# Pinning the SiLU activations of two state-space layers to program order in a four-layer network kernel

## The chip, the cores and the metric

The kernel runs on one core of a Trainium2 chip. The metric is the device time of one execution in microseconds (us), given as the median of three runs; the profile is that of a fourth execution. Five engines with queues of their own do the work: TensorE (PE in the profile, its weight loads apart as PEld), VectorE (DVE), ScalarE (ACT), GpSimd (POOL) and SyncE (SP), on whose queue all DMAs of this kernel are issued.

## The reference, cut to what matters

The input is 16 images of 192 channels and 32 by 32 pixels. Four layers follow each other, each as `x = x + layer(group_norm(x))`: an mLSTM block, a Mamba block, a depthwise convolution, and a two-dimensional selective scan over four directions. The two state-space layers, 1 and 3, hold the part that matters here:

```
xc = silu(depthwise_conv(x_in))                  # 384 channels, 1024 positions
dt = softplus(dt_proj(x_proj(xc)))
h_t = exp(dt_t * A) * h_{t-1} + dt_t * x_t * B_t # 16 states for each channel
y_t = sum_n h_t[n] * C_t[n]
out = layer_norm(y + D * xc) * silu(z)           # layer 3; layer 1 has no norm here
```

In layer 3 the scan runs over each image in four orders (rows, columns, and both reversed), and the four results are added.

## The kernel before, in words

**Stages.** `run` calls `layer0`, `layer12` and `layer3` one after the other. Layer 0 takes about the first 4310 us, layer 1 with layer 2 at its side the next 3800, and layer 3 the last 9830, by the times of the scan instructions of L933 in the trace.

**The scan loop.** `scan_run` walks over *units*. A unit is 512 positions of one image in one scan direction; layer 3 has 8 units for an image, 128 in all. Each unit has 16 *steps*, one for each state n, so an image of layer 3 is 128 steps, and I number them 0 to 127 below. A step holds, for each of three blocks of 128 channels,

- on ACT: `da = exp(dt * A)` (L909), and in three parts `xbt = ut * B` (L889);
- on PE: four small matmuls that turn `xbt` into the scan's layout (L917, L920), and four that add `h * C`, transposed, to the sum y (L951);
- on DVE: the scan itself, `h` (L933);
- on POOL: `h * C` for all three blocks in one instruction (L940).

The buffers between them are few: five of `da`, three of `xb`, four of `h`, two of `xbt`, four of `cb` (the row of C, which a DMA on SP spreads over 128 partitions, L891).

**Side work.** Everything else of a layer is written as Python generators that `Side.tick` advances between the parts of a step, each in a span of steps given where it is added in `layer3`. For an image b of layer 3 these are: `prep` of the next unit, in steps 16j-14 to 16j-3 (it has the softplus: Exp in L841, Ln in L842, three times for a unit); `layer3_columns` of image b-1 in steps 2 to 8; `layer3_tail` of image b-1 in steps 8 to 36; `layer3_local` and `layer3_z` of image b+1 in steps 45 to 78; `layer3_xc` of image b+1 in steps 78 to 112. The tail of the last image runs after the loop.

**The tail.** `layer3_tail` handles an image in two halves of 512 positions. For each it issues a DMA that fetches z back from DRAM into `sz`, which lives in the single buffer `tmp`; normalises v (`layer_norm`: Square L361, Ln L363, Exp L364); calls `self.silu(sz)`; scales v with three activations (L1579); and multiplies v by `sz` on POOL (L1583). After that instruction the second half's DMA (L1574) may refill `tmp`. `tmp` is also the work buffer of `layer3_front` (L1458, L1461) and of `layer3_local` (L1495).

**The activation table.** An activation needs its function's table set in ACT. SiLU is in one set; Exp and Ln are together in another, whose name the kernel keeps as `LNEXP`. The kernel writes a load of that set behind every SiLU (L531 in layer 0, L1207 in layers 1 and 3), and the compiler adds a load ahead of every activation whose function the set in force lacks. All show in the profile as ACT_TABLE_LOAD, under the line of the activation that they serve.

**What sets the order.** The kernel is written for a scheduler that takes the traced instructions and lays out each engine's queue by its own estimate of when inputs are ready; waits come from the data alone. An instruction whose input is there early may so be placed far ahead of where it was traced. Where that is not wanted, an edge can be added that only orders issue: `keep_in_program_order(ins)` puts `ins` behind the instruction traced just before it on the same engine. In `silu` (L1204) that is done for the table load, whose predecessor is the SiLU activation. So the load can't come ahead of the SiLU, but nothing holds the two together, and nothing holds the SiLU to its place. In layer 0 the SiLU activations (L529) are pinned as well. `silu` is called from `layer1_conv`, `layer1_gate`, `layer3_xc` and `layer3_tail`.

Of the kernel before, what the change touches and what calls it, by code (L numbers as in the profile page):

```python
# [11 lines left out]
AF = mybir.ActivationFunctionType  # L12
# [239 lines left out]
class Program:  # L252
# [950 lines left out]

    def silu(self, x):  # L1204

        self.nc.scalar.activation(x, x, AF.Silu)
        self.tc.keep_in_program_order(self.nc.scalar.preload_act_table_set(LNEXP))  # L1207

    def layer1_gate(self, b, bp, psum):
# [424 lines left out]
```

## Time and profile before

| what | value |
|---|---|
| median of 3 runs (lowest to highest) | 17937.86 us (17929.37 to 17949.53) |
| the profiled execution's own time | 17942.07 us |
| its span | 17940.3 us |
| PE busy | 16197.5 us (90%) |
| DVE busy | 13314.9 us (74%) |
| ACT busy | 12215.5 us (68%) |
| POOL busy | 11472.7 us (64%) |
| mean granted TensorE clock | 0.945 |
| scan of layer 3, first to last step | 8112.7 to 17879.1 us |
| one image of layer 3, typical | 611 to 617 us |

The span is the profiled part of that execution, and 1.8 us lie around it. The shares of the whole span mix stages with different loads: ACT is busy for 1166 of the 4310 us of layer 0, but for 8533 of the 9767 us of layer 3's scan, where PE is busy for 8991, DVE for 8490 and POOL for 7894. Such shares can be asked for any stretch of time, and the stretches that count here are a few steps long. In a list of groups each row gives the line, engine and operation, the count after an x, then the busy time in total, the mean duration in ns, and the idle time just before with what ended it.

### The profile page before, as it was taken

What the parts mean: (1) busy time and instruction counts of PE and PEld (TensorE: products, weight loads), DVE (VectorE), ACT (ScalarE), POOL (GpSimd) and SP (SyncE); (2) the same over time, 40 slices, a digit from 0 to 9 for tenths busy, and PEclk for the clock granted to TensorE, in tenths of its full rate; (3) what the DMA queues carried; (4) which work ended last, traced back from release to release, by engine and by line L of the source; (5) the groups of instructions that cost most, each with busy time, mean ns of one, the idle gap of its engine ahead of it and who ended that gap; (6) DMA issues with size and microseconds to landing.
All of it is one profiled execution on the core that took longest, in us unless ns stands there. A gap on an engine that the chain in (4) does not pass through costs nothing.

```text
span 17940.3 us, 264092 instructions
## 1 busy us (share of the span) xinstructions
PE 16197.5 (90%) x99836; PEld 11281.1 (63%) x99836; DVE 13314.9 (74%) x14875; ACT 12215.5 (68%) x19906; POOL 11472.7 (64%) x5556
## 2 busy tenths in 40 slices
PE   8999889898999999979899999999988999999998
PEld 4444444444655555546777777777777777777777
DVE  4444445444777777758888888888888888888888
ACT  2222222223766666647888898888888888988888
POOL 3333333333555555547787888787878877887878
PEclk8898898888999999989999999999999999999999
DMA  1111111112433333333333233333333332333232
GB/s 43 31 32 32 32 32 30 30 31 82 116 115 116 112 117 114 111 107 100 89 101 103 84 97 105 97 90 95 107 91 93 99 105 85 92 105 101 88 93 65
DMA packets 877953, 1511.12 MB, mean 84 GB/s; under 512 B 80336, under 2 KB 311197, under 8 KB 865834
## 3 DMA queue, kind: packets, MB, share of 16 engines
q1 hardware_dynamic: 876682, 1494.22, 28.6%
q8 instruction: 791, 12.96, 0.3%
q14 instruction: 480, 3.93, 0.1%
HBM read 1264.99 MB, written 228.92 MB: 83 GB/s over the span
## 4 chain that ended last, share of the span: by engine, by line
PE 27%; ACT 11%; DVE 8%; issue 4%; POOL 4%; DMA 1%; SPq 0%; POOLq 0%; DVEq 0%; ACTq 0%
PE y L951 7%; PE xb L917 6%; DVE h L933 6%; PE xb L920 4%; ACT da L909 4%; ACT xbt L889 3%; POOL h L940 3%; PE mm L1094 3%; PE mm L810 1%; PE mm L839 1%; PE mm L1517 1%; ACT L909 1%; ACT L842 1%; PE mm L1502 1%; ACT lnsq L842 1%
## 5 line engine op out<-in xcount | busy, mean ns | idle before, releaser
L940 POOL TENSOR_TENSOR h<-h,cb 128x1536 f32<-128x1536 f32 x2560 | 8880.1, 3472 | 1635.0 <-DVE h L933 1045.2
L909 ACT ACTIVATE da<-dt,neg_a 128x512 f32<-128x512 f32 x7680 | 5242.3, 714 | 1542.7 <-DVE h L933 1455.8
L933 DVE TENSOR_TENSOR_SCAN h<-da,carry,xb 128x512 f32<-128x512 f32 x3840 | 4664.9, 1262 | 812.8 <-PE xb L920 605.4
L951 PE MATMUL y<-const,h 128*128 128x128 f32 x30720 | 4739.7, 277 | 132.9 <-DVE ysum L1391 54.6
L933 DVE TENSOR_TENSOR_SCAN h<-da,xb 128x512 f32<-128x512 f32 x3840 | 4439.2, 1202 | 389.9 <-PE xb L920 255.2
L917 PE MATMUL xb<-const,xbt 128*128 128x128 f32 x23040 | 4128.4, 283 | 490.1 <-ACT xbt L889 266.7
L889 ACT ACTIVATE xbt<-ut,bt 128x384 f32<-128x384 f32 x7680 | 4172.9, 603 | 227.5 <-PE xb L917 225.0
L917 PEld LDWEIGHTS xb<-const,xbt 128*128 128x128 f32 x23040 | 2776.7, 143 | 1940.3 <-ACT xbt L889 678.8
L951 PEld LDWEIGHTS y<-const,h 128*128 128x128 f32 x30720 | 3705.2, 144 | 322.9 <-issue 258.8
L920 PE MATMUL xb<-diag,ut 128*128 128x128 f32 x15360 | 3028.5, 279 | 0.0
L920 PEld LDWEIGHTS xb<-diag,ut 128*128 128x128 f32 x15360 | 2400.0, 197 | 68.2 <-issue 68.2
L458 PE MATMUL conv<-ypad,w_conv 96*96 96x512 f32 x2304 | 1253.8, 665 | 3.1 <-ACT y L465 3.1
L899 POOL TENSOR_TENSOR diag<-const,bt 128x512 f32<-128x512 f32 x640 | 668.3, 1044 | 584.7 <-PE xb L920 363.7
L939 POOL COPY carry<-h 128x3 f32<-128x3 f32 x1280 | 255.0, 199 | 1152.2 <-DVE h L933 887.1
L753 POOL TENSOR_TENSOR hs<-h,mhm 128x384 f32<-128x384 f32 x128 | 106.4, 831 | 1027.9 <-DVE den L758 902.0
L636 POOL TENSOR_TENSOR e<-e,const 128x1536 f32<-128x1536 f32 x128 | 444.8, 3475 | 437.3 <-DMA e<-row 406.4
L458 PEld LDWEIGHTS conv<-ypad,w_conv 96*96 96x96 f32 x2304 | 380.4, 180 | 450.1 <-issue 431.1
L839 PE MATMUL mm<-dbl,w_dt 45*128 45x512 f32 x960 | 551.2, 659 | 27.0 <-DVE v L1413 16.1
L638 ACT ACTIVATE e<-e 128x1536 f32<-128x1536 f32 x128 | 189.6, 1482 | 453.9 <-POOL e L637 408.0
L706 PEld LDWEIGHTS num<-v,p 128*128 128x128 f32 x3072 | 433.1, 218 | 78.2 <-issue 55.3
L843 DVE SCALAR_TENSOR_TENSOR dt<-lnsq,mm 128x512 f32<-128x512 f32 x480 | 322.4, 672 | 211.2 <-ACT lnsq L842 210.7
L1094 PE MATMUL mm<-rep,taps 128*32 128x512 f32 x3072 | 428.6, 614 | 27.3 <-DMA rep<-xr 21.4
(272 smaller groups left out, 18026.7 us busy)
## 6 DMA issues: line engine op xcount, KB each, us to landing
cb<-row SPq DMA_DIRECT2D x2560, 256.0 KB
rep<-xr SPq DMA_DIRECT2D x384, 331.0 KB
e<-row SPq DMA_DIRECT2D x128, 768.0 KB
rep<-xin SPq DMA_DIRECT2D x384, 256.0 KB
rep<-xr SPq DMA_DIRECT2D x384, 228.8 KB
x<-x SPq DMA_DIRECT2D x48, 768.0 KB
xr<-xin SPq DMA_DIRECT2D x48, 612.5 KB
xr<-xpad SPq DMA_DIRECT2D x32, 867.0 KB
```

Source lines behind the costliest of these rows:

```text
L458: nc.tensor.matmul(ps[:HP], self.w_c2[:, k, t, m * HP : (m + 1) * HP], yp[:, k, r0 : r0 + 16, t % 3 : t % 3 + W], start=t + k == 0, stop=t ...
L636: nc.gpsimd.tensor_tensor(e, e, self.k0("mask")[:, None, :].to_broadcast([128, NH, 128]), ADD)
L839: nc.tensor.matmul(ps, w_dt[:, t * 128 : (t + 1) * 128], dbl, start=True, stop=True)
L889: nc.scalar.activation(t[:, c], u.ut[:, c], AF.Copy, scale=u.bt[:, c, n : n + 1])
L899: nc.gpsimd.tensor_tensor(d, ident[:, None, :].to_broadcast([128, 4, 128]), u.bt[:, 3, n : n + 4][:, :, None].to_broadcast([128, 4, 128]), ...
L909: nc.scalar.activation(da[i, t], u.dt[:, t], AF.Exp, scale=u.neg_a(t, n))
L917: in_order(nc.tensor.transpose(xb[i, t][:, c * 128 : (c + 1) * 128], xbt[i][:, c, t * 128 : (t + 1) * 128], ident))
L920: in_order(nc.tensor.matmul(xb[i, t][:, 384:], u.ut[:, 3, t * 128 : (t + 1) * 128], u.diag[n // 4][:, n % 4], start=True, stop=True, skip_ ...
L933: nc.vector.tensor_tensor_scan(hv, dv, xv, 0.0 if first else u.carry_in[:, n, t : t + 1], MUL, ADD)
L940: nc.gpsimd.tensor_tensor(h[i], h[i], u.c.pop(n)[:, None, :].to_broadcast([128, 3, 512]), MUL)
L951: in_order(nc.tensor.matmul(u.y[:, j], h[i][:, t, c * 128 : (c + 1) * 128], ident, is_transpose=True, start=n == 0 and j % 4 == 0, stop=n ...
L1094: self.nc.tensor.matmul(ps[32 * g : 32 * g + 32], blocks[:, g * side + r], seen, start=r == 0, stop=r == side - 1, skip_group_check=True,)
```

## The change

The SiLU activation gets the issue-order edge that the table load behind it already has. Its predecessor is whatever was traced last on ACT: in `layer3_tail` the Exp of the layer norm (L364), in `layer1_conv`, `layer1_gate` and `layer3_xc` the last activation that the side work or the scan loop traced. Nothing that is computed changes, and no wait, buffer or DMA is added or removed in the source.

```diff
     def silu(self, x):

-        self.nc.scalar.activation(x, x, AF.Silu)
+        self.tc.keep_in_program_order(self.nc.scalar.activation(x, x, AF.Silu))
         self.tc.keep_in_program_order(self.nc.scalar.preload_act_table_set(LNEXP))
```

## The prediction

> **What bounds the kernel now.** I read the page first, then ACT's groups (the page leaves table loads out), then one image of layer 3 cut into stretches, then ACT's timeline and the waits in the worst stretch. The list of ACT's groups shows the odd thing:
>
> ```profile
> L842 ACT ACTIVATE lnsq<-lnsq,const 128x512 f32<-128x512 f32 x480 | 343.8, 716 | 4.1
> ...
> L909 ACT ACT_TABLE_LOAD x127 | 162.9, 1283 | 2.3
> L842 ACT ACT_TABLE_LOAD x96 | 123.2, 1283 | 1.7
> ...
> L1206 ACT ACT_TABLE_LOAD x80 | 102.6, 1283 | 72.3 <-DMA tmp<-sz 58.3 <-DVE sz L1223 13.0
> L1207 ACT ACT_TABLE_LOAD x80 | 102.6, 1283 | 1.4
> ...
> L363 ACT ACT_TABLE_LOAD x16 | 20.5, 1283 | 0.3
> L841 ACT ACT_TABLE_LOAD x15 | 19.2, 1283 | 0.3
> ```
>
> 80 SiLUs need 80 loads before and 80 behind. The other 127 + 96 + 16 + 15 = 254 loads stand in front of Exp and Ln, which share the set of L1207. So in places that set is not in force, and ACT swaps between a set for Exp and one for Ln. For image 4 (steps counted by L933, three to a step) the stretches are steps 2-17, 18-24, 25-33, 34-49, 82-85, 86-97 and 98-113:
>
> ```profile
> core 0: us, PE busy (x) PEld busy (x) DVE busy (x) ACT busy (x) POOL busy (x), PEclk, DMA share, GB/s
> 10575.50:10656.80 81.30, 71.15 (x507) 57.40 (x505) 71.87 (x73) 66.02 (x114) 63.30 (x36) 0.98 0.23 70
> 10656.80:10711.10 54.30, 41.76 (x224) 31.70 (x225) 32.35 (x32) 52.32 (x74) 34.78 (x13) 0.84 0.18 50
> 10711.10:10749.50 38.40, 36.53 (x275) 30.59 (x274) 38.02 (x38) 34.91 (x60) 32.66 (x13) 1.00 0.32 101
> 10749.50:10823.10 73.60, 63.79 (x468) 53.65 (x467) 71.03 (x78) 59.34 (x104) 62.67 (x37) 0.93 0.36 107
> ...
> 10974.30:11000.60 26.30, 23.45 (x137) 16.46 (x136) 16.67 (x16) 26.13 (x38) 18.11 (x7) 0.94 0.48 145
> 11000.60:11054.20 53.60, 52.87 (x407) 40.09 (x407) 46.04 (x42) 46.69 (x80) 42.03 (x16) 0.97 0.40 123
> 11054.20:11125.10 70.90, 70.46 (x575) 53.78 (x575) 61.36 (x59) 63.90 (x105) 62.08 (x35) 1.00 0.41 125
> ```
>
> The reader is to see who is full: ACT in rows 2 (52.3 of 54.3) and 5 (26.1 of 26.3), DVE in row 3, PE in the last two. Row 2 takes 7.8 us a step, row 3 4.3. ACT's timeline in row 2:
>
> ```profile
> 10657.52 1.28 ACT L1206 ACT_TABLE_LOAD   x1 [3.90 <-DMA tmp<-sz]
> ...
> 10666.18 0.71 ACT L909 ACTIVATE da<-dt,neg_a 128x512 f32<-128x512 f32 x1
> 10666.92 1.28 ACT L842 ACT_TABLE_LOAD   x1
> 10668.21 0.72 ACT L842 ACTIVATE lnsq<-lnsq,const 128x512 f32<-128x512 f32 x1
> 10668.95 1.28 ACT L909 ACT_TABLE_LOAD   x1
> 10670.25 0.72 ACT L909 ACTIVATE da<-dt,neg_a 128x512 f32<-128x512 f32 x1
> ```
>
> and the waits of that stretch, in total, count and longest:
>
> ```profile
> PE xb L917 <- ACT xbt L889: 9.5, 6, 5.4
> ...
> DVE h L933 <- ACT da L909: 3.9, 4, 1.8
> ```
>
> PE and DVE wait for ACT: in these stretches ACT's time is the kernel's time.
>
> **What the Trainium skill says.** "ScalarE: Activation LUTs", section "What ACT_TABLE_LOAD costs": a load takes about 1283 ns and some 1380 ns of drain. The trace agrees on 1283, not on the drain: from the da at 10666.18 to the Ln behind a load 2.03 us pass, and 0.61 pass between ACT instructions without one. A load costs 1.42 us here, and I use that. The same page, "Table sets: the hidden batching unit", says that one set holds Exp and Ln; the trace agrees, since the softplus of steps 99-102 (in the last row) has no load at all. "TensorE: Matmul & The Clock Gate", "Part 1: The HAM clock gate", says that an idle PE gets a slower clock: row 2 has 0.84, full rows 0.97 to 1.00. A gain from that is inside the lengths I compare and not added again.
>
> **The change, part by part.** I compared the order of the instructions in the two built programs, in which there is no time.
>
> *Where it acts.* ACT's order is the same in layers 0 and 1 and up to step 75 of layer 3's first image; every xc SiLU stays at its step. Only the tail's SiLUs move. In image 4's queue the first half's SiLU stands at step 77 before, for a tail 66 steps later, with its L1207 load at 89; the second half's stands at 18.7 with its load at 23.7. Between each pair lie one unit's softplus and, in the second, a layer norm. After, both SiLUs have their load directly behind them, at 15.7 and 23.7.
>
> *Loads removed.* The program has one of the 254 left, so 253 x 1.42 = 359 us of ACT time go (325 busy). For a full image the list gives 8 + 6 + 1 + 1 = 16: 9 in steps 18-23, 6 in 83-85, one at 76. 15 x 16 = 240; 13 more lie in the last image.
>
> *Steps 18-24.* 9 x 1.42 = 12.8 us go. The next limit is far: 54.3 - 12.8 = 41.5 for ACT, against POOL's 34.8, DVE's 32.4 and 224 matmuls at row 3's 0.14 = 31 for PE. All 12.8 pay.
>
> *The stall.* The second SiLU stood first in ACT's queue while its DMA, issued at 10653.3 behind POOL's multiply, landed at 10657.5: 3.9 us an image (58.3 / 15) with all of ACT behind it. After, the DMA is issued one step later but the SiLU comes at 23.7, four steps (over 13 us) later. A landing of 4.2 us is covered, and 3.9 us go.
>
> *The first half's SiLU.* With its two loads it now costs 1.28 + 1.49 + 1.28 and the lost overlap, 4.2 us, in steps 15-16. There the trace has bare steps of 3.33 us that ACT just fills (three da and three xbt take 3.36), so I charge it in full; the low end is 0 if ACT's idle 15 us in row 1 takes it. Queued behind it are the da and xbt of the next step, two v activations (L1579), and through them POOL's multiply. With the stall gone the two nearly cancel: 3.9 - 4.2 = -0.3.
>
> *Sum for steps 2-33:* 12.8 - 0.3 = 12.5; I take 12.0, since row 3 is full on DVE whatever ACT does.
>
> *Steps 82-97.* 6 x 1.42 = 8.5 us leave ACT in row 5. PE is next: at the pace of steps 98-101 (149 matmuls in 19.2 us) 137 take 17.7, and the eight 512-column ones of `layer3_xc` (L1537) some 0.45 each above a small one, 3.6, so 21.3 instead of 26.3: 5.0. From both sides: 0 (if PE's 23.45 of 26.3 is as full as it gets, like row 1's 71.15 of 81.3) to 8.5. The second load that leaves step 89 lies beside a full PE (52.9 of 53.6): nothing. If that cover were gone, 1.4.
>
> *Steps 75-77.* The SiLU and two loads leave, 4.2 us, but PE is busy for 75.9 of 77.5 us in steps 66-81. I take 0.5, at most 1.6.
>
> *The last image* has no next image beside it, so ACT is seldom full: 13 x 1.42 = 18.5, of which I take 8.
>
> *The end.* After the loop nothing covers ACT. The first SiLU now stands between L364 and the v activations, before the second half's Square. That is worth about 4.1, and the multiply, DMA and second SiLU follow as much later: 5 us lost.
>
> *Other moves.* VectorE, PE, POOL and SP see some instructions change places, nearly all within a step or two, and the `tmp` loads on SP move by at most two `cb` loads. Their effect can have either sign; one us an image, 15 in all, bounds it, and I take 0.
>
> Per image 12.0 + 5.0 + 0.5 = 17.5; 15 x 17.5 = 262.5; plus 8, less 5: 265.5. The profiled execution took 17942.07 (span 17940.3 and 1.8 around it), so 17676.5; it lies 4.2 above the median of the runs. Measured from that, 17672. I say 17675.
>
> **The rivals.**
>
> *PE takes over at once.* PE is busy for 92% of an image, and its clock may not hold. Then only PE's visible wait for xbt comes back: 9.5 + 1.1 in rows 2 and 5, 10.6 x 15 = 159, giving 17780. For it: PE is full from step 50 on. Against it: row 2's PE time is stretched by waiting (186 ns a matmul against 133 in row 3).
>
> *All ACT time pays.* 359 + 58 - 15 x 4.2 (the moved SiLU) - 5 = 349, giving 17590. Against it: PE beside steps 82-97.
>
> *The loads are hidden or stay.* The build shows them gone, and ACT full; 17930 at best for this case.
>
> *Slower.* ACT's queue is strict. A pinned SiLU whose `tmp` load is late holds every da and xbt. It needs the gain undone and 0.2% more: (265 + 36) / 15 = 20 us of stall an image, so a load landing 33 us after its issue instead of 4.2. At 22 us it would give 17942 + 15 x 22 - 265 = 18007. The DMA share of 0.18 in row 2 speaks against it.
>
> **How the numbers follow.** Forecast 0.68, PE takes over 0.15, all pays 0.12, no effect 0.03, slower 0.02. 0.2%, 36 us, is about what a measurement of this kernel can tell from no change. The first three are all faster: 0.95. The range: the 12.5 of steps 2-33 may be 10 to 14, the 5.0 may be 0 to 8.5 (mostly 3 to 7), the other moves 15: 17620 to 17740 for the forecast alone, and drawn out towards the two rivals 17600 to 17775.
>
> **What would show it.** Right: table loads at L909, L842, L841 gone and one at L363; ACT's busy time down by 325 to some 11890; no idle before L1206 for tmp<-sz; steps 18-24 near 42 us, 82-85 near 21; an image near 596. Wrong: steps 18-24 still above 48 with PE or POOL full, a new wait of L1579 or L1583, or a DMA in front of L1206.

## The result and the profile after

| | before | after |
|---|---|---|
| median of 4 runs each | 17943.6 us | 17739.32 us (17724.52 to 17751.62) |
| ratio, 95% interval | | 0.9887 (0.987 to 0.9904) |
| the profiled execution's own time | 17942.07 us | 17751.62 us |
| ACT busy | 12215.5 us | 11899.2 us |
| mean length of an image of layer 3, images 0 to 14 | 613.7 us | 602.7 us |
| last image | 561.4 us | 533.4 us |

The kernel is faster by 1.1%: 204 us by the medians, 190 us between the two profiled executions. The forecast was 17675, a gain of 265 us. The list of ACT's groups after the change has its table loads in seven rows; left out here are four that are as before (L529, L531, L361, L364):

```profile
L1206 ACT ACT_TABLE_LOAD x80 | 102.6, 1283 | 14.2 <-DVE sz L1223 13.0
L1207 ACT ACT_TABLE_LOAD x80 | 102.6, 1283 | 1.2
...
L363 ACT ACT_TABLE_LOAD x1 | 1.3, 1283 | 0.0
```

The loads at L909, L842 and L841 are gone, one is left at L363, and in front of L1206 there is no idle time for `tmp<-sz` any more. So the change does what it says. The first five of the prediction's seven stretches of image 4, in the same order, are steps 2-17, 18-24, 25-33, 34-49 and 82-85:

```profile
core 0: us, PE busy (x) PEld busy (x) DVE busy (x) ACT busy (x) POOL busy (x), PEclk, DMA share, GB/s
10524.80:10606.80 82.00, 72.94 (x514) 58.20 (x513) 72.12 (x72) 69.84 (x117) 64.13 (x37) 0.98 0.23 64
10606.80:10651.60 44.80, 35.38 (x222) 25.78 (x221) 31.44 (x32) 41.12 (x67) 35.73 (x12) 0.96 0.25 83
10651.60:10688.90 37.30, 35.58 (x273) 30.21 (x272) 36.92 (x34) 32.72 (x56) 30.48 (x13) 1.00 0.26 80
10688.90:10769.40 80.50, 65.00 (x470) 55.56 (x469) 75.63 (x81) 61.26 (x106) 63.11 (x36) 0.92 0.34 103
...
10919.30:10940.70 21.40, 20.86 (x137) 14.71 (x136) 16.36 (x17) 20.52 (x36) 17.88 (x7) 1.00 0.55 181
```

The reader is to see three things. Steps 18-24 (row 2) fell from 54.3 to 44.8 us and PE's clock rose there from 0.84 to 0.96. Steps 82-85 fell from 26.3 to 21.4, and PE is now full in them (20.86). And row 4, steps 34-49, in which this image never had a table load, grew from 73.6 to 80.5 us; DVE's busy time in it grew by 4.6 us. That is a give-back, and the larger part of what the forecast missed. The lengths of the stretches, from the starts of the scans on DVE, as means over images 1 to 15:

| steps | before | after | second half pinned only | loads back | ReLU to PSUM | SiLU inside the norm | before, front late |
|---|---|---|---|---|---|---|---|
| 2-17 | 81.2 | 81.9 | 81.1 | 82.1 | 82.1 | 79.8 | 81.1 |
| 18-24 | 55.8 | 44.7 | 43.9 | 53.7 | 44.6 | 39.9 | 55.4 |
| 25-33 | 38.4 | 37.6 | 37.5 | 37.5 | 34.8 | 44.2 | 35.1 |
| 34-49 | 74.4 | 79.9 | 79.3 | 78.6 | 80.6 | 73.8 | 84.8 |
| 66-81 | 76.8 | 75.6 | 76.8 | 75.5 | 75.5 | 75.6 | 76.7 |
| 82-97 | 77.0 | 71.6 | 77.1 | 75.3 | 71.5 | 71.5 | 76.7 |

Image 15, the last, has table loads in steps 34-65 before the change and loses them, which hides a part of the growth in the row 34-49: in images 2 to 14 alone it is 74.4 to 81.3.

Step by step, a second give-back shows inside row 2: steps 18 to 23 together became 14.5 us shorter (means of images 2 to 14), but step 24 grew from 7.65 to 11.56. PE's queue stands there at the tail's output matmul (L1591) until POOL has multiplied v by sz (L1583), and behind it stand the matmuls that DVE's next scan needs; in image 4 that scan waits 3.3 us before the change and 7.3 after. These are the rows of ACT, DVE, POOL and PE around it, before:

```profile
10703.82 0.80 ACT L1579 ACTIVATE v<-v,p 128x512 f32<-128x512 f32 x1
...
10701.11 1.28 DVE L933 TENSOR_TENSOR_SCAN h<-da,carry,xb 128x512 f32<-128x512 f32 x1
10703.57 0.75 DVE L1594 SCALAR_TENSOR_TENSOR xt<-mm,re,xt 96x512 f32<-96x512 f32 x1 [1.17 <-PE mm L1591]
10704.24 1.27 DVE L933 TENSOR_TENSOR_SCAN h<-da,carry,xb 128x512 f32<-128x512 f32 x1
...
10702.53 3.47 POOL L940 TENSOR_TENSOR h<-h,cb 128x1536 f32<-128x1536 f32 x1 [1.02 <-issue]
10705.96 3.43 POOL L1583 TENSOR_TENSOR v<-v,tmp 128x1536 f32<-128x1536 f32 x1
...
10709.44 1.10 PE L1591 MATMUL mm<-v,w_out 128*96 128x512 f32 x2 [2.71 <-POOL v L1583]
```

and after:

```profile
10640.37 0.80 ACT L1579 ACTIVATE v<-v,p 128x512 f32<-128x512 f32 x1
...
10638.43 0.75 DVE L1594 SCALAR_TENSOR_TENSOR xt<-mm,re,xt 96x512 f32<-96x512 f32 x1 [1.52 <-PE mm L1591]
10639.10 1.27 DVE L933 TENSOR_TENSOR_SCAN h<-da,carry,xb 128x512 f32<-128x512 f32 x1
10640.59 1.28 DVE L933 TENSOR_TENSOR_SCAN h<-da,carry,xb 128x512 f32<-128x512 f32 x1 [0.22 <-ACT da L909]
...
10640.50 3.47 POOL L940 TENSOR_TENSOR h<-h,cb 128x1536 f32<-128x1536 f32 x1 [3.11 <-issue]
10643.92 3.44 POOL L1583 TENSOR_TENSOR v<-v,tmp 128x1536 f32<-128x1536 f32 x1
...
10647.42 2.02 PE L1591 MATMUL mm<-v,w_out 128*96 128x512 f32 x2 [4.55 <-POOL v L1583]
...
10649.66 1.48 PE L1591 MATMUL mm<-v,w_out 128*96 128x512 f32 x2
```

It would be natural to blame ACT, where the second SiLU with its two loads now stands right ahead of the v activations. But the last of these ends 1.3 us before POOL's multiply starts in the first kernel and 2.7 us in the second, so POOL does not wait for it. POOL goes to the tail's multiply straight from its h multiply (L940), and that starts 0.13 or 0.14 us after the third scan of step 23 has ended. This scan (10701.11 before, 10639.10 after) now stands in DVE's queue behind the tail's L1594, which waits for PE; before, it stood ahead of it. So, counted from the first scan of step 24 (10704.24 and 10640.59), the multiply starts at 3.3 us instead of 1.7. And four output matmuls instead of two now stand ahead of the ones that the next scan needs: 3.5 us of PE's rows instead of 1.1. In images 2 to 15 the order is the same. This give-back comes of new places in the queues of DVE and PE.

For the first give-back the order of the built program and two timelines say where to look. In image 4's queues the front's second pair of ReLU (L1461) and min-and-add (L1464) stands at step 40 after the change, and stood at step 34 before. DVE and POOL in step 40 of the changed kernel:

```profile
10713.26 1.21 DVE L933 TENSOR_TENSOR_SCAN h<-da,xb 128x512 f32<-128x512 f32 x1
10714.39 0.67 DVE L328 BATCH_NORM_STATS2 gnst<-x 96x6 f32<-96x512 f32 x1
10714.98 3.47 DVE L1464 SCALAR_TENSOR_TENSOR x<-tmp,x 96x512 f32<-96x512 f32 x1
```

```profile
10714.46 3.44 POOL L940 TENSOR_TENSOR h<-h,cb 128x1536 f32<-128x1536 f32 x1
```

POOL's multiply ends at 10717.90, and the min-and-add, 0.66 us of work, ends 0.55 us after it. The Trainium skill says in "SBUF — State Buffer", section "Who interferes with whom", that a VectorE instruction with two SBUF inputs contends with a GpSimd instruction that reads SBUF. Both inputs of L1464 are in SBUF. The trace agrees: in the changed kernel 30 of the 64 min-and-adds take over 1 us, each starts inside POOL's L940, and each ends 0.54 or 0.55 us after it. The scans take one input from PSUM; 4541 of layer 3's start inside a long POOL instruction, and none takes over 1.29 us.

### The profile page after: what moved, and what is told of

Same layout as the page of the kernel before. It is cut to its first block, busy times and chain, and to the rows that moved or that the text cites. A ratio compares the mean times of both kernels' runs of the same rounds, so it can differ in the third digit from the quotient of the medians.

```text
span 17749.8 us, 263742 instructions
## 1 busy us (share of the span) xinstructions
PE 16096.1 (91%) x99836; PEld 11228.6 (63%) x99836; DVE 13328.7 (75%) x14875; ACT 11899.2 (67%) x19653; POOL 11473.1 (65%) x5556
## 5 line engine op out<-in xcount | busy, mean ns | idle before, releaser
L940 POOL TENSOR_TENSOR h<-h,cb 128x1536 f32<-128x1536 f32 x2560 | 8875.0, 3470 | 1429.5 <-DVE h L933 883.9
L909 ACT ACTIVATE da<-dt,neg_a 128x512 f32<-128x512 f32 x7680 | 5266.5, 714 | 1737.1 <-DVE h L933 1668.3
L917 PE MATMUL xb<-const,xbt 128*128 128x128 f32 x23040 | 4076.6, 282 | 419.3 <-DVE h L933 263.2
L1094 PE MATMUL mm<-rep,t_dw 96*32 96x512 f32 x2304 | 434.7, 614 | 22.6 <-DMA rep<-xr 16.3
```

The lines of the kernel that those rows point to most:

```text
L909: nc.scalar.activation(da[i, t], u.dt[:, t], AF.Exp, scale=u.neg_a(t, n))
L917: in_order(nc.tensor.transpose(xb[i, t][:, c * 128 : (c + 1) * 128], xbt[i][:, c, t * 128 : (t + 1) * 128], ident))
L940: nc.gpsimd.tensor_tensor(h[i], h[i], u.c.pop(n)[:, None, :].to_broadcast([128, 3, 512]), MUL)
L1094: self.nc.tensor.matmul(ps[32 * g : 32 * g + 32], blocks[:, g * side + r], seen, start=r == 0, stop=r == side - 1, skip_group_check=True,)
```

## The experiments

My theory after the result: a reload costs ACT 1.42 us and pays in full in steps 18-24 and up to PE's limit in 82-97; two things are given back, by the front's min-and-add in step 40 and by what I then took for a late multiply in step 24. The rivals: PE bounds the kernel whatever ACT does, or the gain is that of the SiLU's place and not of the loads. Each kernel is compared with runs of the kernel before on its own chip; differences between kernels are taken from the ratios, times 17940. By the intervals of the ratios such a difference is uncertain by some 35 us.

**Only the second half pinned.**

```diff
-    def silu(self, x):
+    def silu(self, x, pin=True):

-        self.tc.keep_in_program_order(self.nc.scalar.activation(x, x, AF.Silu))
+        ins = self.nc.scalar.activation(x, x, AF.Silu)
+        if pin:
+            self.tc.keep_in_program_order(ins)
...
-            self.silu(sz)
+            self.silu(sz, i == 1)
```

> The tail's second SiLU and all other SiLUs are pinned as in the changed kernel, the tail's first one is not. In the built order it floats back to step 76 of the image before, and the six reloads of steps 82-85 are there again; the nine of steps 18-23 stay gone and the front's order of steps 34-41 is that of the changed kernel. My theory (each group of reloads pays where ACT is full): steps 66-97 go back to the lengths of before, +6.6 us an image, -0.7 for steps 15-16, so about +90 us against the changed kernel: 17830. Rival (PE is the bound in steps 82-97 whatever ACT does): same as the changed kernel, 17740. Rival (all the gain sat in 82-97): 17930.

Measured: 17825.24 us, ratio 0.9941 (0.9929 to 0.9954), so about 97 us slower than the changed kernel. Steps 82-97 are back at 77.1, steps 66-81 at 76.8, and steps 18-24 stay short. The six reloads of the second group are worth some 5.5 us an image, and PE is not a bound that hides them. The last image has its 13 loads back too and takes 14 us longer. The opposite edit, only the first half pinned, gives the changed kernel's order of instructions but for a few in the very last tail, so it was not run.

**The loads put back, the SiLUs left in place.**

```diff
             nc.scalar.activation(e, ps, AF.Exp)
+            again = getattr(u, "reload", False)
+            if again:
+                self.tc.keep_in_program_order(nc.scalar.preload_act_table_set(LNEXP))
             nc.scalar.activation(e, e, AF.Ln, bias=self.k("one"))
+            if again:
+                self.tc.keep_in_program_order(nc.scalar.preload_act_table_set(LNEXP))
...
                         u.k = k
+                        u.reload = j == 0 and k >= 2
```

> The changed kernel with the SiLUs where it has them, and a superfluous load of the Exp and Ln set before and after each Ln of two units of an image of layer 3 (the units of steps 18-23 and 82-85): 12 loads an image, 192 in all. My theory (a load costs ACT 1.42 us, and ACT is full there): steps 18-24 longer by 8.5 us, 82-97 by 5.4, so 16 x 13.9 = 220 us: 17960. Rival (the gain came from the SiLU's new place and the stall that is gone, not from the loads): 17740. Rival (PE hides most of it): 16 x 5 = 80 us: 17820.

Measured: 17944.23 us, ratio 1.0006 (0.9998 to 1.0015): the whole gain is gone, about 213 us for 192 loads, where 220 was expected. With the columns as above, image 4's steps 18-24 and 82-85 of this kernel:

```profile
10658.20:10712.40 54.20, 41.41 (x223) 30.25 (x222) 32.28 (x33) 49.39 (x73) 35.67 (x12) 0.81 0.24 68
10979.60:11005.70 26.10, 24.41 (x156) 14.94 (x155) 17.77 (x18) 25.92 (x38) 17.34 (x7) 1.00 0.52 172
```

They have the lengths of before (54.3 and 26.3), although SiLUs, stall and the front's place are those of the changed kernel, and PE's clock in steps 18-24 falls to 0.81 again. In the means steps 18-24 are 9.0 us longer for six loads, 1.5 us each. So it is the loads that count, and not the SiLUs' new place. What the stall that is gone was worth by itself was not measured.

**The front's ReLU into PSUM.**

```diff
+                ps = psum.tile([128, 512], F32, name="mm")
                 nc.scalar.activation(
-                    y2[:, h], y2[:, h], AF.Relu, bias=self.bn2[:, m, 1:2], scale=self.bn2[:, m, 0:1]
+                    ps[:HP], y2[:, h], AF.Relu, bias=self.bn2[:, m, 1:2], scale=self.bn2[:, m, 0:1]
                 )
-                nc.vector.scalar_tensor_tensor(x[:, m, h], y2[:, h], 6.0, x[:, m, h], MIN, ADD)
+                nc.vector.scalar_tensor_tensor(x[:, m, h], ps[:HP], 6.0, x[:, m, h], MIN, ADD)
```

> The changed kernel, but the front's ReLU writes into PSUM, so that the min-and-add of L1464 reads one operand from PSUM and one from SBUF; it still stands at steps 39-40. Theory A (that instruction, with two SBUF operands, is held until POOL's multiply has ended): its longest falls from 3.48 us to under 0.8, and steps 34-49 lose some 4 us an image: 17680. Theory B (the clump of four DVE instructions in one step is the cost, whoever runs beside it): durations and steps 40-41 stay, 17740.

Measured: 17707.73 us, ratio 0.9876 (0.9863 to 0.989); the interval overlaps that of the changed kernel, so the time alone tells little. The instruction tells more. Its row (least, median and longest ns) in the changed kernel and in this one:

```profile
L1464 DVE SCALAR_TENSOR_TENSOR x<-tmp,x x64: 656/728/3480, 7995.5 to 16745.1; 96x512 f32<-96x512 f32 x64
```

```profile
L1465 DVE SCALAR_TENSOR_TENSOR x<-mm,x x64: 659/664/689, 7984.9 to 16696.4; 96x512 f32<-96x512 f32 x64
```

Of the 64, 48 start inside POOL's L940, with at least 0.64 us of it to run, and none is held. So theory A is right on the mechanism. On the time theory B is nearer: steps 40 and 41 fell by 6.6 us, but all four instructions now stand at 38.7 to 40.3, steps 38 and 42 grew by 3.1 and 2.9, and 25-49 together only fell from 117.5 to 115.4. The kernel has also moved two more of the four instructions late than the changed kernel had, so it does not take the holding away alone.

**The SiLU inside the norm.**

```diff
-            yield from self.layer_norm(bp, psum, vs, vs, self.k("ones384"), 128, 512)
+            norm = self.layer_norm(bp, psum, vs, vs, self.k("ones384"), 128, 512)
+            yield next(norm)
             self.silu(sz)
+            yield from norm
```

> The changed kernel, with the tail's SiLU traced after the first part of the layer norm instead of behind all of it. In the built order the SiLUs stand at 12.3 and 20.3 instead of 15.7 and 23.7, the v activations stay, and the front's min-and-add is back at steps 31-34. My theory (two things were given back: the front's move into step 40, some 6 us an image, and the late multiply on POOL for which PE waits in step 24, 3.9 us): both return, 15 x 10 = 150 us, 17590. Rival (PE bound, the lengths of 24 and 34-49 come from elsewhere): 17740. Rival (the second SiLU now waits for its DMA at 20.3 as before the change): 3.9 us an image lost again, 17650.

Measured: 17645.52 us, ratio 0.9843 (0.9829 to 0.9856), 79 us faster than the changed kernel, half of what was expected. Step 24 fell from 11.56 to 4.18 us, and PE's wait for the tail's multiply from 17 times and 77.0 us to twice and 11.9, but not because the multiply comes earlier. In image 4 step 24 starts at 10629.47, and POOL and PE show

```profile
10632.90 3.48 POOL L1585 TENSOR_TENSOR v<-v,tmp 128x1536 f32<-128x1536 f32 x1
...
10642.32 1.45 PE L1593 MATMUL mm<-v,w_out 128*96 128x512 f32 x3
```

The multiply starts 3.4 us into the step, as late as in the changed kernel. But the first output matmul that needs it now stands so far back in PE's queue that it starts at 12.9 us, and PE does not wait for POOL there. Step 24 is shorter than even in the kernel before (7.65). So its length is set by where those matmuls stand in PE's queue, and my reason for this part of the forecast was wrong.

Steps 34-49 are back at 73.8. But the front's instructions are now held in steps 30-33 instead: by 62 us beyond their free duration in steps 25-33, over all images, where the changed kernel has 16. Steps 25-33 grew from 37.6 to 44.2, which is more than that: the first give-back moved and did not go.

**The front late, in the kernel before.**

```diff
-                nc.vector.scalar_tensor_tensor(x[:, m, h], y2[:, h], 6.0, x[:, m, h], MIN, ADD)
+                self.tc.keep_in_program_order(
+                    nc.vector.scalar_tensor_tensor(x[:, m, h], y2[:, h], 6.0, x[:, m, h], MIN, ADD)
+                )
```

> The kernel before, with one edge more: the front's min-and-add (L1464) is kept in program order on VectorE, so that its four instructions stand at steps 39-41 instead of 31-34; SiLUs and table loads stay as they are. My theory (the front's move alone was a give-back of the change, some 6 us an image): steps 34-49 longer by 6 to 8 us, 15 images, 18030. Rival (those steps got longer for another reason that came with the change): 17930.

Measured: 17999.78 us, ratio 1.0055 (1.0042 to 1.0068): 98 us slower than the kernel before, without any pinned SiLU. Steps 34-49 grew by 10.4 us and 25-33 fell by 3.3, 7.1 together. This is a larger move than that of the changed kernel: here all four instructions go to steps 37.3 to 41.0, there only the second pair goes, from 33.7 and 34.0 to 40.0 and 40.3, and steps 25-49 grow by 6.0 in images 2 to 14. For that pair alone image 1 is the better witness. It has the pair at 39.7 and 40.0 in both kernels, and its steps 34-49 take 81.1 us before and 80.7 after, while images 2 to 14 go from 74.4 to 81.3. So a late front costs time whatever the SiLU does.

**The SiLU ahead of the norm.**

```diff
             vs = [v[:, t, h] for t in range(3)]
-            yield from self.layer_norm(bp, psum, vs, vs, self.k("ones384"), 128, 512)
+            yield Wait(1.5)
             self.silu(sz)
+            yield from self.layer_norm(bp, psum, vs, vs, self.k("ones384"), 128, 512)
```

> The changed kernel, with the tail's SiLU traced ahead of the whole layer norm: in the built order at steps 11.0 and 18.7 (12.3 and 20.3 in the variant inside the norm), with its load behind it; the second half's DMA is issued no earlier. Theory (a SiLU at 18.7 meets the DMA that is still under way, and ACT stands still as it did before the change): a wait of L1206 for tmp<-sz of 4 to 8 us an image, so 60 to 120 us slower than the variant inside the norm, 17705 to 17765. Rival (the landing is covered): as that variant, 17645.

Measured: 17640.05 us, ratio 0.9847 (0.9834 to 0.9861), the same as inside the norm. The wait did come. ACT's L1206 waits for `tmp` 15 times and 98.4 us in all, 6.6 us an image, and steps 18-24 are 5.8 us longer than in the former (45.7 against 39.9). But steps 25-33 are 3.7 and steps 2-17 1.5 shorter. The front's instructions meet POOL less (30 us beyond their free duration in the whole run instead of 65), which is 2.3 us an image; where the rest comes from was not looked into. The forecast of the wait was right and that of the time wrong.

**Inside the norm, and the ReLU into PSUM.** The edits are the two above together.

> The SiLU inside the norm, and the front's ReLU into PSUM. Theory: the min-and-add (65 us of excess beside POOL in the former) is no longer held; its place goes to steps 39-40 as in the PSUM variant alone, so the gain of that one (30 us) adds: 17615. Rival (the two give-backs are the same time and do not add): 17645.

Measured: 17565.51 us, ratio 0.981 (0.9796 to 0.9823), 59 us faster than the SiLU inside the norm alone. With the holding gone, steps 25-33 are at 35.1 instead of 44.2; the front stands at steps 38 to 40 again, and steps 34-49 are at 79.4 instead of 73.8.

**The group norm's small operations from PSUM too.**

```diff
-        nc.vector.tensor_tensor(d, mv[:, :, 0], mean, SUB)
+        nc.vector.tensor_tensor(d, mv[:, :, 0], ps[:HP, :2], SUB)
         q = pool.tile([HP, 2], F32, name="gnq")
-        nc.vector.tensor_tensor(q, d, d, MUL)
-        nc.vector.tensor_tensor(q, q, mv[:, :, 1], ADD)
+        nc.vector.tensor_tensor(ps[:HP, 2:4], mv[:, :, 0], ps[:HP, :2], SUB)
+        nc.vector.tensor_tensor(ps[:HP, 2:4], ps[:HP, 2:4], d, MUL)
+        nc.vector.tensor_tensor(q, ps[:HP, 2:4], mv[:, :, 1], ADD)
```

> As the one before, and the group norm's three small subtractions and products (96 x 2) each take an operand from PSUM. Theory (they too are held by POOL, 2.4 to 2.7 us for 0.15 us of work, some 70 us in all in the PSUM variant, in steps in which VectorE is the fullest engine): half of it shows, 17580. Rival (VectorE has room there): 17615.

Measured: 17512.63 us, ratio 0.9782 (0.9769 to 0.9795), 50 us faster than without it; of these some 30 lie in steps 34-49, now at 77.4. What is gone are rows like these, of the kernel with the ReLU in PSUM: the subtraction ends with POOL's multiply.

```profile
10710.33 2.70 DVE L336 TENSOR_TENSOR gnd<-gnmv,gnmean 96x2 f32<-96x2 f32 x1
...
10709.56 3.45 POOL L940 TENSOR_TENSOR h<-h,cb 128x1536 f32<-128x1536 f32 x1
```

This version beats both kernels: 2.2% under the one before.

## Why the prediction was right, and where it was not

*Where it acts, and the loads removed.* Right: 253 loads are gone, and ACT's busy time fell by 316 us where 325 was forecast. The price of 1.42 us a load held: putting 192 back cost 213 us, 1.1 us each over all, and 1.5 in steps 18-24.

*Steps 18-24 and the stall.* The terms 12.8 and 3.9 less 4.2 for the moved SiLU made 12.5 for steps 2-23. Measured is a gain of 14.5 in steps 18-23, less the 0.6 by which 2-17 grew: 13.9. The sum of the three was nearly right; which of them was off was not measured one by one, but steps 2-17 grew by far less than the 4.2 that the moved SiLU was charged there.

*Steps 82-97.* Right: 5.0 forecast, 5.4 measured, with PE full afterwards. Steps 66-81: 0.5 forecast, 1.2 measured.

*Other moves.* This step failed. "One us an image, 15 in all, bounds it, and I take 0" was said of the instructions that change place, on the ground that nearly all move by a step or two. The steps into which two such moves fall grew by 145 us in all in the changed kernel.

The first is the front's second pair, from step 34 to step 40: steps 34-49 grew by 91 us in images 0 to 14 together. Not all of it is the holding. The trace of before already had the warning: 31 of the 64 min-and-adds started during a POOL instruction and took 1.43 us in the median instead of 0.66; after the change 57 do. But what they take beyond 0.66 us grew only from 5 to 41 us in steps 34-49, all images together. The rest comes with the place, where the front's work now bunches with the scans; how, the runs do not take apart.

The second is in step 24, which grew by 54 us in all images together: DVE's L1594 ahead of a scan, and two more output matmuls in PE's queue where it waits for POOL. The prediction had named "a new wait of L1579 or L1583" as a sign of being wrong. PE's wait for L1583 grew from 52.2 to 77.0 us, and it did not come through the v activations, where the prediction looked for it.

*The last image.* 8 us were taken for its own 13 loads. It became 28.0 us shorter, of which 11.8 in steps 18-24 belong to the tail's group and 17.3 to these 13 loads (steps 34-65), nearly their full price of 18.5; with these loads back in the kernel that pins the second half only, the image takes 14 us longer again. "ACT is seldom full" there was wrong.

*The end.* 5 us forecast, 4.0 measured: from the last scan to the end 61.2 us became 65.2.

The sum, from the starts of the scans in the two traces, all images together (gains positive):

| where | forecast | measured |
|---|---|---|
| steps 2-23 and 25-33 | 180 | 223 |
| step 24 | 0 | -54 |
| steps 34-49, images 0 to 14 | 0 | -91 |
| steps 34-65, last image | 8 | 17 |
| steps 66-97 | 82 | 108 |
| all other steps, and before layer 3 | 0 | -9 |
| the end | -5 | -4 |
| all | 265 | 190 |

So the time fell into the stated range in part by luck: the other terms paid some 80 us more than forecast, and that made up for about half of what the moves took back.

The rival "PE takes over at once" came within 41 us of the time, but not by its mechanism: PE is busy for only 35.4 of 44.8 us in steps 18-24, and six loads put back there lengthen them by 9.0 us. Why the scheduler moved these instructions when the SiLU was pinned was not looked into; the order is a fact of the two builds, the reason stays open.

## What to carry to other kernels

An activation that needs another table set, and the load that brings the common set back, belong together in the queue; here only the load was tied down, and the Exp and Ln that fell between the two reloaded in turn. When an edit lets a scheduler lay out the queues anew, compare the new place of every instruction of the fullest engine, and ask of each VectorE instruction with two inputs in SBUF whether it now falls beside a long GpSimd one. Ask the same of every instruction that waits for another engine, like the output matmul here: what stands behind it in its queue waits too.

## What the runs showed of the hardware that I had not expected

A VectorE instruction on two SBUF operands does not slow down beside GpSimd's multiply but stands until it has ended: 3.47 us for 0.66, and up to 2.71 us for a subtraction of 96 x 2 elements that takes 0.16 us at its fastest. With one operand in PSUM the same min-and-add took at most 0.69 us, 48 times beside GpSimd's multiply. And a table load left no drain behind it: 1.28 us of load and 0.14 us of lost overlap between two ACT instructions, and 1.5 us for each load put back where ACT was full, not the 2.66 that the Trainium skill gives for a switch in "ScalarE: Activation LUTs", section "What ACT_TABLE_LOAD costs".
